# Graph layer on one Trainium2 core: SyncE fetches one gather unit in 60 instead of one in 72, node blocks travel in twos, and the store rounds of a pack become single steps

## The chip, the cores and the metric

The kernel runs on one core of one Trainium2 chip. The metric is the device time of one execution in microseconds (us); lower is better. Engine names are those of the profile: PE is TensorE (PEld its weight loads), DVE is VectorE, ACT is ScalarE, POOL is GpSimd, SP is SyncE. SP does no arithmetic here: it is a queue that issues transfers, in the order of the program.

## What is computed

One residual graph layer with a layer norm. There are 50,000 nodes of 160 numbers each (64 scalars and 32 vectors of 3) and 1,650,000 edges sorted by destination; 50,000 of them are self loops.

```python
ss, vv = (s[src], v[src])                       # the row of x at each edge's source
out0 = C0 * (ss * e0 @ W1 + dot * INV3 @ W2)    # products with the edge's 4 numbers
m = jnp.concatenate([out0, out1.reshape(-1, 3 * MUL1)], axis=1)
m_agg = jax.ops.segment_sum(m, dst, num_segments=n)
h = ...                                         # m_agg times Ws and Wv
x = _layernorm(x + relu(h))
```

## The kernel before

**Units, groups, pairs, sections.** The edges are taken in units of 128. For each unit, 128 rows of `x` must be gathered, one into each partition. Six units make a group (`G`), two groups a pair (`PG = 2`), twenty groups a section (`SG = 20`). So a pair is 12 units and a section is 10 pairs; there are 1,044 pairs and 12,522 units. The main loop (line 800) runs over pairs.

**One pair.** `gather` (line 314) has POOL fetch the rows, one indirect transfer for each unit, into a tile `xg`; the pool `rows` has four such tiles (`bufs=4`). `spread` (line 324) has VectorE make `ha`, the edge's four numbers put in the column of its destination (128 x 1536); it has three buffers, and is made for pair p+1 while pair p is in hand. `group_sums` (line 336) multiplies: twelve products (24 matmul records) of `ha` and `xg` into the PSUM tile `ps` (two buffers), and then VectorE transposes `ps` into `sums` (line 349). An `xg` tile is free again when TensorE has used it.

**Sections.** Every ten pairs `load` (line 247) has SP bring in the next section's edges, `cast` (line 265) has ScalarE make the byte offsets `ro`, and `place` (line 278) has TensorE and VectorE put them in place. The `ha` of the pairs of a section need its `place`.

**Help from SyncE.** SP fetches some units itself (`fetch`, line 665): it loads 32 offsets into registers and issues 32 transfers of one row of 640 bytes, four such batches to a unit, into a tile `xr` of the pool `far`. `HELP = {ET.SP: 72}` means one unit in 72. Lines 647 to 661 deal the four batches out over pairs (`at`) and name the pair `q` that uses the unit; here `q` is two pairs after the last batch. POOL leaves that unit out.

**Packs.** The self loops have to be taken out of the edge list. That is done in 16 packs of 128 rows of 790 edges (`pack`, line 408), one for about 60 pairs of the main loop. A pack is a list of steps: read, begin, 131 VectorE instructions (lines 438 to 528: compares, a scan, and shifts by `copy_predicated`), and 17 store rounds (`store`, line 539), each of which loads offsets into registers and issues up to 16 transfers from SP. The main loop deals a pack's steps evenly over the pairs up to its due time (lines 834 to 842); a `None` in the list is a step with nothing in it. The due pairs are 39, 99, 159, 229, 289 and so on.

**Node blocks.** 391 blocks of 128 nodes are finished along the way: `ahead` (SP loads `x` and the self-loop numbers), `own`, `nodes`, `block` (TensorE and VectorE), the norm in `norm1` to `norm3`, and `do_send` (SP writes the result). They are called a fixed number of pairs after the sums that they need (lines 794 to 798 and 843 to 850).

**Order.** Line 799 holds SP to the order of the program. The order on the other engines is made by a scheduler when the program is built, and every engine then works through its own list in order:

```python
        later_pools.enter_context(tc.manual_schedule(engines={ET.SP}))
        for p, (s, g, ng) in enumerate(pairs):
```

So an instruction of a pack may stand on VectorE's list ahead of, or behind, where its step was dealt.

Of the kernel before, what the change touches and what calls it, by code (L numbers as in the profile page):

```python
# [38 lines left out]
F32 = mybir.dt.float32  # L39
# [6 lines left out]
ET = mybir.EngineType  # L46
# [3 lines left out]
P = 128  # L50
MUL0, MUL1 = 64, 32
D = MUL0 + 3 * MUL1
NK = 4
# [13 lines left out]
PG = 2  # L67
SG = 20

HELP = {ET.SP: 72}  # L70
HEAD = 100
RP = 128
RS = 16
KM = 31
# [29 lines left out]
def tile_gnn_resnorm(ctx: ExitStack, tc: tile.TileContext, x, src, dst, attr, W1, W2, W3, W4, W5, Ws, Wv, out, n_edges):  # L104
    nc = tc.nc
    N = x.shape[0]
    NBLK, NB, GA, G, NU, NG, L, NH, NR, FAR = plan(N, n_edges)
# [83 lines left out]
    def norm2(pool, mv, n):  # L191
        rstd = pool.tile([P, 1], F32, name="rstd")
        nc.scalar.activation(rstd[:n], mv[:n, 1:2], AF.Sqrt, bias=eps_t[:n])  # L193
        return rstd

    def norm3(pool, y, mv, rstd, n):
        nc.vector.reciprocal(rstd[:n], rstd[:n])
        o = pool.tile([P, D], F32, name="o")
        nc.vector.tensor_scalar(o[:n], y[:n], mv[:n, 0:1], rstd[:n], op0=ALU.subtract, op1=ALU.mult)  # L199
        return o  # L200

# [14 lines left out]
    nblocks = math.ceil(N / P)  # L216
# [7 lines left out]

    with tc.tile_pool(name="once", bufs=1) as once, tc.tile_pool(name="raw", bufs=2) as rawp, \
            tc.tile_pool(name="idx", bufs=2) as idxp, tc.tile_pool(name="rows", bufs=4) as rowp, \
            tc.tile_pool(name="far", bufs=3) as farp, \
            tc.tile_pool(name="ops", bufs=3) as op, tc.tile_pool(name="sums", bufs=4) as sump, \
            tc.tile_pool(name="hp", bufs=alive + 4) as hpp, tc.tile_pool(name="node", bufs=3) as np_, \
            tc.tile_pool(name="ahead", bufs=7) as aheadp, \  # L230
            tc.tile_pool(name="psC", bufs=1, space=PSUM) as psC, tc.tile_pool(name="psK", bufs=2, space=PSUM) as psK, \
            tc.tile_pool(name="psP", bufs=1, space=PSUM) as psP, tc.tile_pool(name="psA", bufs=2, space=PSUM) as psA, \
            tc.tile_pool(name="psM", bufs=2, space=PSUM) as psM, ExitStack() as later_pools:
# [8 lines left out]
        dq = nc.sync  # L242
# [115 lines left out]
        def row_start(r):  # L358

            lo, hi = (math.floor(r * L * (1 - 1 / degree)) - 2 * FAR - 2, math.ceil(r * L * (1 - 1 / degree)) + 2 * FAR + 2)  # L360
            return (max(lo, 0), hi if r else 0), (max(math.floor((EH + r * L) / degree) - FAR - 2, 0),
                                                  math.ceil((EH + r * L) / degree) + FAR + 2)

        edges = dram.tile([1, (row_start(NR - 1)[0][1] + L) * C], F32, name="edges")
        selves = dram.tile([1, (row_start(NR - 1)[1][1] + W) * NK], F32, name="selves")
        edge_bytes = edges.bitcast(U8).rearrange("o f -> (o f)")
        self_bytes = selves.bitcast(U8).rearrange("o f -> (o f)")
        rows_stored = [0]
# [39 lines left out]
        def pack(c):  # L408

            r0 = c * RP  # L410
            n = min(RP, NR - r0)
            e0 = EH + r0 * L
            e = slice(e0, e0 + n * L)
            steps, T = [], {}
# [154 lines left out]


            for head, j in [(False, j) for j in range(RS)] + [(True, 0)]:
                steps += [partial(store, head, j), None, None, None]
            return steps + [stored]

        def apply_weights(at, ng):
# [8 lines left out]
        def rows_of(b):  # L584
            nb = min(P, N - b * P)
            return nb, slice(b * P, b * P + nb)

        def ahead(b):

            nb, row = rows_of(b)  # L590
            xt = aheadp.tile([P, D], F32, name="xt")
            dq.dma_start(xt[:nb], x[row, :])

            assert rows_stored[0] == NR or row_start(rows_stored[0])[1][0] >= row.stop
            sa = aheadp.tile([P, NK], F32, name="sa")
            dq.dma_start(sa[:nb], selves[0, row.start * NK:row.stop * NK].rearrange("(n k) -> n k", k=NK))
            return xt, sa

        def nodes(b):

# [47 lines left out]
        for h, (eng, period) in enumerate(HELP.items()):  # L648
            first = PG * G + h * period // 2
            nbatch = P // ROWS[eng]  # L650
            while True:
                at = [int(first + i * period / nbatch) // (PG * G) for i in range(nbatch)]
                q = at[-1] + 2
                if q >= len(pairs) or pairs[q][2] < PG:
                    break
                s, g, ng = pairs[q]
                u = (g - s * SG + ng) * G - 1 - len(helped.get(q, []))
                helped.setdefault(q, []).insert(0, (eng, h))
                for i, p in enumerate(at):
                    batches.setdefault(p, []).append((eng, h, q, s, u, i))  # L660
                first += period
# [54 lines left out]
                of_nodes[b] += (nodes(b),)  # L716

        def do_ahead(b):
            of_nodes[b] = ahead(b)

        def do_own(b):
            of_nodes[b] = own(b, *of_nodes.pop(b))
# [5 lines left out]
            rstds[b] = norm2(np_, resid[b][1], rows_of(b)[0])  # L728

        def do_store(b):  # L730
            outs[b] = norm3(np_, *resid.pop(b), rstds.pop(b), rows_of(b)[0])

        def do_send(b):
            nb, row = rows_of(b)
            dq.dma_start(out[row, :], outs.pop(b)[:nb])

        def do_cast(s):
            raws[s] = cast(raws[s])
# [179 lines left out]
    with tc.tile_pool(name="edges2", bufs=2) as ep, tc.tile_pool(name="ops2", bufs=2) as op, \  # L918
            tc.tile_pool(name="node2", bufs=1) as np_, tc.tile_pool(name="psA2", bufs=2, space=PSUM) as psA, \
            tc.tile_pool(name="psF2", bufs=1, space=PSUM) as psF:  # L920
        with tc.For_i(0, blocks, 1) as b:
            u0 = table(0, b)
            u1 = table(1, b)
            acc = np_.tile([NBLK, NK, D], F32, name="acc")
            nc.vector.memset(acc, 0.0)

            with tc.For_i(u0, u1, GA) as u:
                u = nc.s_assert_within(u, 0, NU - GA, skip_runtime_bounds_check_because="below u1")
                s_t = ep.tile([P, GA], I32, name="s_t")
                d_t = ep.tile([P, GA], I32, name="d_t")  # L930
                a_t = ep.tile([P, GA, NK], F32, name="a_t")
                e = ds(u * P, GA * P)
                nc.sync.dma_start(s_t, src1[e].rearrange("(p j) o -> p (j o)", j=GA))
                nc.sync.dma_start(d_t, dst1[e].rearrange("(p j) o -> p (j o)", j=GA))
                nc.sync.dma_start(a_t, attr[e].rearrange("(p j) k -> p j k", j=GA))
                rel = ep.tile([P, GA], F32, name="rel2")
                nc.vector.tensor_scalar(rel, d_t, base[:, ds(b, 1)], None, op0=ALU.subtract)
                xg = op.tile([P, GA, D], F32, name="xg2")
                for j in range(GA):
                    nc.gpsimd.indirect_dma_start(  # L940
                        out=xg[:, j, :], out_offset=None, in_=x,
                        in_offset=bass.IndirectOffsetOnAxis(ap=s_t[:, j:j + 1], axis=0))
                hot = op.tile([P, GA, NBLK], F32, name="hotb")
                nc.vector.tensor_tensor(hot, slots[:, :NBLK].unsqueeze(1).to_broadcast([P, GA, NBLK]),
                                        rel.unsqueeze(2).to_broadcast([P, GA, NBLK]), op=ALU.is_equal)
                xa = op.tile([P, GA, NK, D], F32, name="xa")
                nc.vector.tensor_mul(xa, xg.unsqueeze(2).to_broadcast([P, GA, NK, D]),
                                     a_t.unsqueeze(3).to_broadcast([P, GA, NK, D]))
                ps = psA.tile([NBLK, 2, 512], F32, name="ps2")
                for j in range(GA):  # L950
                    for h in range(2):
                        nc.tensor.matmul(ps[:, h, 0:2 * D], hot[:, j, :], xa[:, j, 2 * h:2 * h + 2, :],
                                         start=j == 0, stop=j == GA - 1)
                nc.vector.tensor_add(acc.rearrange("n (h k) f -> n h (k f)", h=2),
                                     acc.rearrange("n (h k) f -> n h (k f)", h=2), ps[:, :, 0:2 * D])
            parts = []
            for h in range(2):
                pt = psF.tile([D // 2, NK, P], F32, name="pt2")
                for k in range(NK):
                    nc.tensor.transpose(pt[:, k, :NBLK], acc[:, k, h * (D // 2):(h + 1) * (D // 2)], ident[:NBLK, :NBLK])  # L960
                at = np_.tile([D // 2, NK, NBLK], F32, name=f"ac{h}")
                nc.scalar.copy(at, pt[:, :, :NBLK])
                parts.append(at)
            ph = psF.tile([NBLK, D], F32, name="ph2")
            i = 0
            for h, at in enumerate(parts):
                for k in range(NK):
                    nc.tensor.matmul(ph, at[:, k, :], BWh[:, h, k, :], start=i == 0, stop=i == 2 * NK - 1)
                    i += 1
            row = ds(b * NBLK, NBLK)  # L970
            xt = np_.tile([NBLK, D], F32, name="xt2")
            nc.scalar.dma_start(xt, x[row, :])
            y, mv = norm1(np_, ph, xt, NBLK)
            o = norm3(np_, y, mv, norm2(np_, mv, NBLK), NBLK)
            nc.scalar.dma_start(out[row, :], o[:NBLK])


# [31 lines left out]
```

## Time and profile before

| | |
|---|---|
| median of 10 runs | 15,677.5 us (15,669.83 to 15,679.73) |
| the profiled execution's own time | 15,675.17 us |
| its span, first to last instruction | 15,673.4 us |
| POOL, share of the span | 75%, 12,363 instructions |
| PE | 51% |
| DVE | 40% |
| ACT | 3% |
| 16 DMA engines, mean | about 30%, 78 GB/s |

In the profile "L319" is line 319 of the kernel. A group reads: line, engine, operation, output from inputs, shape, count, then busy time and mean ns of one instruction, then the idle time of the engine just before them and what ended it. A timeline row reads: start, duration, what, and in brackets the idle time before it and its releaser. Of POOL, the time in which the gather's issue is prepared counts as idle, "issue".

### The profile page before, as it was taken

How to read it: one execution, taken by the hardware profiler on the slowest of the kernel's cores; microseconds unless marked ns; L12 is line 12 of the kernel's file. 1: busy time of each engine (PE TensorE's matmuls, PEld its weight loads, DVE VectorE, ACT ScalarE, POOL GpSimd, SP SyncE). 2: the span in 40 equal slices, each digit the busy share in tenths (PEclk: the TensorE clock that was granted, in tenths of full speed). 3: DMA queues.
4: the chain of work that ended last, by engine and by line, in shares of the span. 5: the costliest groups of instructions: out<-in, count | busy, mean ns of one | idle time of the engine just before them, and what ended most of it. 6: DMA issues, size and time to landing. Idle time of an engine off the chain costs nothing. (4 is left out here: it accounts for less than half of the span.)

```text
span 15673.4 us, 167279 instructions
## 1 busy us (share of the span) xinstructions
PE 8002.8 (51%) x38505; PEld 7272.1 (46%) x38506; DVE 6238.8 (40%) x11070; ACT 537.3 (3%) x1497; POOL 11694.9 (75%) x12363
## 2 busy tenths in 40 slices
PE   4555544554555445454554555555555455555555
PEld 3444444444444444444454444444444444444444
DVE  5342525225253442524435243352433525234322
ACT  0000000000000000000000000000000000000000
POOL 7777777777777777777777777777777777777776
PEclk7777777777777777777777777777777777777777
DMA  3323233332333323333233332323333233332322
GB/s 80 86 74 83 71 79 77 77 84 73 78 79 78 82 73 79 80 78 82 72 79 79 78 82 73 83 73 77 82 76 83 74 80 78 78 80 72 77 73 66
DMA packets 843237, 1218.89 MB, mean 78 GB/s; under 512 B 300227, under 2 KB 623912, under 8 KB 838262
## 3 DMA queue, kind: packets, MB, share of 16 engines
q0 software_dynamic: 592752, 1012.42, 26.2%
q1 hardware_dynamic: 248058, 194.45, 4.4%
q8 instruction: 323, 5.29, 0.1%
q14 instruction: 664, 5.44, 0.1%
q10 hardware_dynamic: 1440, 1.29, 0.0%
HBM read 1135.77 MB, written 71.40 MB: 77 GB/s over the span
## 5 line engine op out<-in xcount | busy, mean ns | idle before, releaser
L319 POOL DMA_INDIRECT xg<-in_x,si x12349 | 11690.7, 947 | 3933.9 <-issue 3716.4
L343 PE MATMUL ps<-xg,ha 128*128 128x160 f32 x24698 | 5310.2, 392 | 6197.7 <-DMA xg<-in_x,si 5293.9
L343 PEld LDWEIGHTS ps<-xg,ha 128*128 128x128 f32 x24698 | 5075.8, 267 | 6418.0 <-issue 5511.9
L349 DVE STREAM_TRANSPOSE sums<-ps 128x320 f32<-128x320 f32 x1044 | 535.9, 513 | 6021.2 <-PE ps L343 5939.8
L331 DVE TENSOR_TENSOR ha<-hot,pk 128x1536 f32<-128x1536 f32 x1044 | 1801.8, 1727 | 727.7 <-PE ps L343 702.3
L579 PE MATMUL phc<-BWk,sums 128*128 128x160 f32 x5220 | 923.7, 330 | 786.7 <-DVE sums L349 680.3
L579 PEld LDWEIGHTS phc<-BWk,sums 128*128 128x128 f32 x5220 | 825.8, 211 | 862.2 <-DVE sums L349 723.2
L623 PE MATMUL yx<-BWh,xT 80*128 80x320 f32 x3128 | 1003.9, 467 | 176.1 <-ACT xT L617 175.3
L627 DVE TENSOR_SCALAR t<-yx,sa 128x160 f32<-128x160 f32 x391 | 149.6, 383 | 1845.9 <-PE yx L623 1824.0
L623 PEld LDWEIGHTS yx<-BWh,xT 80*128 80x128 f32 x3128 | 598.0, 201 | 471.0 <-ACT xT L617 263.3
L639 PE MATMUL phb<-hp,hot 128*128 128x160 f32 x3474 | 605.2, 323 | 302.2 <-DVE t L629 301.4
L639 PEld LDWEIGHTS phb<-hp,hot 128*128 128x128 f32 x3474 | 536.4, 206 | 398.4 <-issue 392.4
L328 DVE TENSOR_TENSOR hot<-bank,rel 128x384 f32<-128x384 f32 x1044 | 555.1, 546 | 4.1
L629 DVE SCALAR_TENSOR_TENSOR t<-yx,sa,t 128x160 f32<-128x160 f32 x1173 | 448.2, 382 | 130.8 <-PE yx L623 105.7
L617 ACT COPY xT<-ptx 80x256 f32<-80x256 f32 x391 | 143.8, 368 | 10395.6 <-PE ptx L615 10094.5
L511 DVE COPY_PREDICATED prow<-marks,prow 128x2370 f32<-128x2370 int32 (+8 forms) x160 | 443.5, 2772 | 0.6
L511 DVE COPY_PREDICATED pra<-marks,pra 128x1580 f32<-128x1580 int32 (+8 forms) x160 | 305.0, 1907 | 0.0
L605 DVE TENSOR_TENSOR hot<-bank,rr 128x512 f32<-128x512 f32 (+2 forms) x391 | 288.3, 737 | 0.0
L640 DVE TENSOR_TENSOR phb<-phb,t 128x160 f32<-128x160 f32 x391 | 129.8, 332 | 362.4 <-PE phb L639 358.2
L581 ACT COPY hp<-phc 128x160 f32<-128x160 f32 x522 | 150.2, 288 | 2908.3 <-PE phc L579 2895.4
L193 ACT ACTIVATE rstd<-mv,eps_t 128x1 f32<-128x1 f32 x391 | 115.2, 295 | 1729.5 <-DVE mv L188 1708.2
L615 PE MATMUL ptx<-ident,xt 128*80 128x128 f32 (+1 forms) x782 | 160.0, 289 | 0.0
(148 smaller groups left out, 2858.0 us busy)
## 6 DMA issues: line engine op xcount, KB each, us to landing
xr<-in_x SPq DMA_DIRECT2D x22144, 0.6 KB
xg<-in_x,si POOLq DMA_INDIRECT x12349
edges<-prow SPq DMA_DIRECT2D x1994, 18.5 KB
r<-edges SPq DMA_DIRECT2D x99, 360.0 KB
selves<-mine SPq DMA_DIRECT2D x1992, 0.5 KB
xt<-in_x SPq DMA_DIRECT2D x390, 80.0 KB
out<-o SPq DMA_DIRECT2D x390, 80.0 KB
pra<-in_attr SPq DMA_DIRECT2D x15, 1580.0 KB
```

The source lines that it names most:

```text
L319: got.append(nc.gpsimd.indirect_dma_start(out=xg[:, j, :], out_offset=None, in_=x, in_offset=bass.IndirectOffsetOnAxis(ap=placed[0][:, u + ...
L328: nc.vector.tensor_tensor(hot[:, :n], slotsP[:, 0:W].unsqueeze(1).to_broadcast([P, n, W]), rel[:, u:u + n].unsqueeze(2).to_broadcast([P, n ...
L331: nc.vector.tensor_tensor(ha[:, :n], hot[:, :n].unsqueeze(2).to_broadcast([P, n, NK, W]), pk[:, :, u:u + n].rearrange("p k u -> p u k").un ...
L343: mm = nc.tensor.matmul(ps[:, j // G, :], ha[:, j].rearrange("p k w -> p (k w)"), xr, start=j % G == 0, stop=j % G == G - 1)
L349: nc.vector.transpose(at[:, :, i:i + ng, :].rearrange("p b g w -> p g b w"), ps[:, :ng].rearrange("p g (b f) -> p g b f", f=FB))
L511: nc.vector.copy_predicated(what[:n, a:e], mi[:, r].unsqueeze(2).to_broadcast([n, e - a, what.shape[2]]), what[:n, a + d:e + d])
L579: nc.tensor.matmul(ph[:ng * W], at[:, b, :ng].rearrange("p g w -> p (g w)"), BWk[:, b, :], start=b == 0, stop=b == ND - 1)
L605: nc.vector.tensor_tensor(hot2[:, :len(cs)], slotsP.unsqueeze(1).to_broadcast([P, len(cs), P]), rr[:, :len(cs)].unsqueeze(2).to_broadcast( ...
L615: nc.tensor.transpose(pt[:, i, :nb], xt[:nb, i * H:(i + 1) * H], ident[:nb, :nb])
L623: nc.tensor.matmul(y[:nb], xT[:, i, :nb], BWh[:, i, ks, :], start=i == 0, stop=i == 1)
L629: nc.vector.scalar_tensor_tensor(t[:nb], y[:nb, i], sa[:nb, k:k + 1], t[:nb], op0=ALU.mult, op1=ALU.add)
L639: nc.tensor.matmul(ph[:nb], hot2[:r, i, :nb], hp[:r], start=i == 0, stop=i == len(cs) - 1)
```

## The change

Six edits, in one change:

- one unit in 60 is fetched by SP (`HELP`), in the same batches of 32 rows;
- the pair that uses the unit is five pairs after the last batch (it was two); no unit is fetched for the last ten pairs; a batch is asked for no earlier than the third pair of the section before;
- the tile pool of the fetched units has four buffers (it had three);
- two node blocks share one load of `x`, one load of the self-loop numbers and one store of the result; the pool `ahead` has 5 buffers instead of 7, and the result has a pool of its own with three buffers of two blocks;
- a store round of a pack is one step; before, it was one step and three empty ones;
- `norm3` writes into a tile that it is given.

```diff
-HELP = {ET.SP: 72}
+HELP = {ET.SP: 60}
+BP = 2
...
-            tc.tile_pool(name="far", bufs=3) as farp, \
+            tc.tile_pool(name="far", bufs=4) as farp, \
...
-            tc.tile_pool(name="ahead", bufs=7) as aheadp, \
+            tc.tile_pool(name="ahead", bufs=5) as aheadp, tc.tile_pool(name="outs", bufs=3) as outp, \
...
             for head, j in [(False, j) for j in range(RS)] + [(True, 0)]:
-                steps += [partial(store, head, j), None, None, None]
+                steps.append(partial(store, head, j))
             return steps + [stored]
...
-        def ahead(b):
-
-            nb, row = rows_of(b)
-            xt = aheadp.tile([P, D], F32, name="xt")
-            dq.dma_start(xt[:nb], x[row, :])
...
+        def together(b):
+
+            bs = list(range(b // BP * BP, min(nblocks, b // BP * BP + BP)))
+            return bs if all(rows_of(i)[0] == P for i in bs) else [b]
+
+        def ahead(bs):
+
+            nb = rows_of(bs[0])[0]
+            n0, n1 = rows_of(bs[0])[1].start, rows_of(bs[-1])[1].stop
+            xt = aheadp.tile([P, BP, D], F32, name="xt")
+            dq.dma_start(xt[:nb, :len(bs)], x[n0:n1, :].rearrange("(h n) d -> n h d", h=len(bs)))
...
                 at = [int(first + i * period / nbatch) // (PG * G) for i in range(nbatch)]
-                q = at[-1] + 2
-                if q >= len(pairs) or pairs[q][2] < PG:
+                q = at[-1] + 5
+                if q >= len(pairs) - 10:
                     break
                 s, g, ng = pairs[q]
+                at = [max(a, (s - 1) * (SG // PG) + 2) for a in at]
...
         def do_store(b):
-            outs[b] = norm3(np_, *resid.pop(b), rstds.pop(b), rows_of(b)[0])
+            bs = together(b)
+            if b == bs[0]:
+                outs[b] = outp.tile([P, BP, D], F32, name="o")
+            norm3(outs[bs[0]][:, b - bs[0]], *resid.pop(b), rstds.pop(b), rows_of(b)[0])
 
         def do_send(b):
-            nb, row = rows_of(b)
-            dq.dma_start(out[row, :], outs.pop(b)[:nb])
+            bs = together(b)
+            if b == bs[-1]:
+                n0, n1 = rows_of(bs[0])[1].start, rows_of(b)[1].stop
+                dq.dma_start(out[n0:n1, :].rearrange("(h n) d -> n h d", h=len(bs)),
+                             outs.pop(bs[0])[:rows_of(b)[0], :len(bs)])
```

More of the change, by code (lines that the diff above doesn't have):

```diff
@@ L194, in norm2, with norm3 @@
         return rstd
-    def norm3(pool, y, mv, rstd, n):
+    def norm3(o, y, mv, rstd, n):
         nc.vector.reciprocal(rstd[:n], rstd[:n])
-        o = pool.tile([P, D], F32, name="o")
         nc.vector.tensor_scalar(o[:n], y[:n], mv[:n, 0:1], rstd[:n], op0=ALU.subtract, op1=ALU.mult)
@@ L586, in rows_of @@
             return nb, slice(b * P, b * P + nb)
-        def ahead(b):
-            nb, row = rows_of(b)
-            xt = aheadp.tile([P, D], F32, name="xt")
-            dq.dma_start(xt[:nb], x[row, :])
[L594 to L597, printed above, removed]
+        def together(b):
[6 more added lines that the diff above has]
+            dq.dma_start(xt[:nb, :len(bs)], x[n0:n1, :].rearrange("(h n) d -> n h d", h=len(bs)))
+            assert rows_stored[0] == NR or row_start(rows_stored[0])[1][0] >= n1
+            sa = aheadp.tile([P, BP, NK], F32, name="sa")
+            dq.dma_start(sa[:nb, :len(bs)],
+                         selves[0, n0 * NK:n1 * NK].rearrange("(h n k) -> n h k", h=len(bs), k=NK))
+            return [(xt[:, h], sa[:, h]) for h in range(len(bs))]
         def nodes(b):
@@ L718, in do_ahead @@
         def do_ahead(b):
-            of_nodes[b] = ahead(b)
+            bs = together(b)
+            if b == bs[0]:
+                of_nodes.update(zip(bs, ahead(bs)))
         def do_own(b):
@@ L730, in do_store @@
         def do_store(b):
-            outs[b] = norm3(np_, *resid.pop(b), rstds.pop(b), rows_of(b)[0])
+            bs = together(b)
+            if b == bs[0]:
+                outs[b] = outp.tile([P, BP, D], F32, name="o")
+            norm3(outs[bs[0]][:, b - bs[0]], *resid.pop(b), rstds.pop(b), rows_of(b)[0])
         def do_send(b):
-            nb, row = rows_of(b)
-            dq.dma_start(out[row, :], outs.pop(b)[:nb])
+            bs = together(b)
+            if b == bs[-1]:
+                n0, n1 = rows_of(bs[0])[1].start, rows_of(b)[1].stop
+                dq.dma_start(out[n0:n1, :].rearrange("(h n) d -> n h d", h=len(bs)),
+                             outs.pop(bs[0])[:rows_of(b)[0], :len(bs)])
         def do_cast(s):
@@ L973, in tile_gnn_resnorm @@
             y, mv = norm1(np_, ph, xt, NBLK)
-            o = norm3(np_, y, mv, norm2(np_, mv, NBLK), NBLK)
+            o = np_.tile([P, D], F32, name="o")
+            norm3(o, y, mv, norm2(np_, mv, NBLK), NBLK)
             nc.scalar.dma_start(out[row, :], o[:NBLK])
```

## The prediction

> **What bounds the kernel now.** I read the page first, then the waits of POOL, then the timelines of POOL, DVE and PE around one of its long waits, then SP's. The page's group of the gather and POOL's waits:
>
> ```profile
> L319 POOL DMA_INDIRECT xg<-in_x,si x12349 | 11690.7, 947 | 3933.9 <-issue 3716.4
> ```
>
> ```profile
> POOL xg L319 <- issue: 3716.4, 12192, 0.6
> POOL xg L319 <- PE ps L343: 164.1, 22, 23.3
> ```
>
> The reader is to see that POOL does nothing else and hardly waits: 947 ns busy and 3716.4/12192 = 305 ns of issue make a gather every 1.252 us, and 12,349 x 1.252 = 15,461 us of the 15,673. The first gather starts at 9.4, the last ends at 15,629, and 44 us of arithmetic and the last stores follow. What is left is waiting, and most of it is one entry, 164 us for PE. In POOL's timeline this falls into 15 long waits of 4 to 23 us, about 900 us apart, together 157 us beyond the normal step. One of them, in the timelines of POOL, DVE and PE:
>
> ```profile
> 1806.33 0.95 POOL L319 DMA_INDIRECT xg<-in_x,si  x1 [0.30 <-issue]
> 1827.52 0.94 POOL L319 DMA_INDIRECT xg<-in_x,si  x1 [20.25 <-PE ps L343]
> ```
>
> ```profile
> 1726.73 1.73 DVE L331 TENSOR_TENSOR ha<-hot,pk 128x1536 f32<-128x1536 f32 x1
> 1728.39 0.57 DVE L506 TENSOR_TENSOR pri<-hit,marks 128x411 int32<-128x411 int32 x1
> ...
> 1815.88 0.36 DVE L199 TENSOR_SCALAR o<-y,mv,rstd 128x160 f32<-128x160 f32 x1
> ...
> 1819.41 1.75 DVE L331 TENSOR_TENSOR ha<-hot,pk 128x1536 f32<-128x1536 f32 x1
> ```
>
> ```profile
> 1821.21 6.04 PE L343 MATMUL ps<-xg,ha 128*128 128x160 f32 x24 [3.43 <-DVE ha L331]
> ```
>
> The reader is to see a chain. VectorE ends one `ha` at 1728.5 and starts the next at 1819.4; between them stand 59 instructions of a pack. PE has gathered rows but no `ha` until 1821.2. POOL has filled all four `xg` tiles by 1807 and waits until PE frees one. So the kernel is POOL's count of gathers plus, once a pack, what a block of pack work on VectorE overruns the four tiles.
>
> **How long a block may be.** Measured gaps between those two `ha` and the excess of POOL's wait, packs 2 to 4: 79.6 gives 8.6, 90.9 gives 19.9, 85.3 gives 13.7. So about 71 us are free and each further us is a us of POOL. The free time has two parts: `ha` is finished 33 to 35 us before POOL completes its pair, and three more pairs of 15 us less the 7.5 us from `ha` to the freed tile are covered by tiles (34 + 37.5). In packs 5 to 7 VectorE came to its block later (lead 21), and 67.0, 69.5, 67.0 gave 7.3, 12.5, 7.5: the same sum.
>
> **Part one, the gathers.** The rule for `q` with 72 and 2 gives 173 units (22,144 rows / 128); with 60, 5 and the last ten pairs left out it gives 205. POOL's list in the built program has 12,317 gathers: 32 fewer, 32 x 1.252 = -40.1 us, all on the path.
>
> **Part two, where the pack's VectorE work comes to stand.** Scheduler and dealing decide this, so I take it from the order of VectorE's list in the built program, and the durations from the rows of this trace. A pack has 131 such instructions in both. Before, in the third pack, 19, 9, 3, 5, 9, 12, 6, 3, 5, 1 and 59 of them stand between one `ha` and the next; after, 12, 2, 3, 6, 5, 6, 2, 3, 2, 5 and 85. The last block grows. By the rows, all work in it takes 80.0 us before (measured gap 90.9) and 99.0 after. Over the packs the block is 99.0 us seven times, 103.9 twice, 108.6 once, 97.2 in the first pack, and 84.6 to 86.9 in five whose `ha` before has already 25 to 29 us ahead of it; before it was 77, 80, 76, then 58 to 59 with 30 to 36 ahead, 46 twice.
>
> From rows to gap: outside waits over 0.8 us, the measured gaps are about 0.97 of the row sums (rows overlap a little). The waits add 4 to 24 us before, median 11; I take 7 after, since pack instructions now stand between the steps of a node block and cover its returns from PE and ACT. So 99.0 x 0.97 + 7 = 103.
>
> Free time after: the `ha` ahead of the block now stands 7.7 us of work behind the transpose that it follows, not 2.8, so the lead falls by 5, and one of the three pairs holds a fetched unit, 1.25 less of gathering. 71 - 5 - 1 = 65. Each of the seven costs 38 us, together 266; the 103.9 and 108.6 blocks 82 and 45; the five, with leads of 19 to 23, 29 to 34 each, together 157; the first 31. Sum 581, against 157 now: +424 us.
>
> The ends: with waits of 4 in every block, 16 x 3 less, 533; with 24, 16 x 17 more, 853. Nothing in the rows lets the block cost less than its own work allows, 99.0 x 0.97 - 71 = 25 a pack or 400 in all.
>
> The Trainium skill has a rule that speaks against longer VectorE work: "SBUF — State Buffer", section "SBUF: two separate sides", says that a VectorE instruction in a two-port mode keeps GpSimd from writing the descriptors of its transfers. This trace does not show it: inside the block, 1728 to 1806, gathers follow each other every 1.250 us, and from 2800 to 2900, without pack work, every 1.251. By the page's 620 against 3100 ns, some 20 more gathers of each pack would be 2.5 us later, an estimate of 800 us over 16 packs; by the rows, 0.
>
> **Part three, SyncE.** A batch of 32 rows takes 10.4 us and 2.5 to load offsets; a store round, from the end of one batch:
>
> ```profile
> 8062.68 10.72 SPq L676 DMA_DIRECT2D xr<-in_x  x32
> 8074.79 0.29 SPq L563 DMA_DIRECT2D edges<-prow  x1
> ...
> 8080.84 0.23 SPq L563 DMA_DIRECT2D selves<-mine  x1
> ```
>
> 7.7 us, loads included. 128 more batches are 1,650 us. SP's own waits show room for them over the run, before its stores of results:
>
> ```profile
> SPq L735 <- DVE o L199: 2963.0, 145, 62.4
> ```
>
> The two-block transfers take away 3 x 195 issues of about 0.4, 234 us of SP time that nobody waits for: nothing. But the store rounds move: with 77 steps instead of 128 in a pack, the 17 rounds stand in 13.4 pairs instead of 32. There SP needs 17 x 7.7 + 10.7 x 12.9 + 5 = 274 us and has 13.4 x 14.75 = 198: it falls 76 us, 5 pairs, behind. Queued behind are the read of the next pack, the next section's edges and the fetches. The fetched unit is asked for 5 pairs ahead, and PE's list has its product behind the next pair's, so it is there in time. Edges and pack data come about 5 pairs later than now: SP stands 1.5 to 3 pairs behind POOL there today, and by the same four-tile sum I find some 27 us left. I take 0, and keep up to 15 us for each of 15 packs, 225, for the range. Below 0 it can't be, since SP comes later, never earlier.
>
> One more buffer for the units, and the earliest pair, change nothing: with 60 the users are pairs 9, 14, 19 and so on, their first batch 8 pairs before, which is inside the bound. The end after the last gather keeps its 44 us.
>
> **Sum.** Against the profiled execution, 15,675.2 (2.3 under the median): -40 + 424 = 16,059. I say 16,060.
>
> **Rivals.**
> - Faster: VectorE's blocks cost no more than now. If the scheduler's blocks found ScalarE or PE late in the old place and not in the new, or VectorE came to them earlier, POOL's waits stay at 157 and only the gathers count: 15,635; without any wait 15,478. It decides at a gap of about 75. Against it: the rows alone give 96. Chance 0.06 with all faster cases.
> - No change: the waits grow by just the 40 us saved; a gap of 78. Chance 0.03.
> - Slower by more: the store rounds are the new bound. If SP falls 7 pairs behind instead of 5, every pack gets a second wait; each pair of lag beyond that is 15 us x 15 packs = 225 us, so 16,285 for one pair and 16,510 for two. For it: the 76 us short. Against it: SP now waits before its stores, and 27 us are left. Chance 0.17.
> - My forecast, 15,880 (400 us of waits) to 16,330 (853) by its own ends: 0.74.
>
> The other cause that the change could seem to aim at, fetched units that come too late, is not in the trace: the 15 long waits all end with an `ha`.
>
> **Numbers.** The range is the forecast's own, 15,880 to 16,330; one pair of lag beyond seven, 16,285, lies inside it. Faster or slower by over 0.2%, 31 us, is about what a measurement can tell from no change: 0.06, 0.03, 0.91.
>
> **What would show it.** Right: 12,317 gathers at 1.25 us; POOL's wait for PE near 580 us in some 16 waits of 30 to 45; gaps of about 103 us between the two `ha`. Part three is wrong if a second wait follows each pack's stores, some ten pairs before the block, with SP's issue of the read seven pairs late. All is wrong if the gaps stay under 75 us.

## The result and the profile after

The kernel after takes 16,036.9 us, median of 8 runs (16,032.7 to 16,045.5), against 15,676.7 us for the kernel before (28 runs, 15,669.8 to 15,682.5). The ratio is 1.023, 95% interval 1.0221 to 1.0239. The profiled execution took 16,040.5 us, its span is 16,038.7. The forecast was 16,060.

The page's group of the gather, and the waits of POOL (total us, times, longest) in the kernel after:

```profile
L319 POOL DMA_INDIRECT xg<-in_x,si x12317 | 11657.8, 946 | 4353.6 <-issue 3704.2
```

```profile
POOL xg L319 <- issue: 3704.2, 12152, 0.3
POOL xg L319 <- PE ps L343: 435.4, 24, 47.5
POOL xg L319 <- PE ptx L622: 167.0, 14, 35.2
```

The count is the expected one and a gather still takes 946 + 305 ns. The waits for PE have grown from 164 to 435 + 167 = 602 us, the longest from 23 to 47. The second entry is no second mechanism: in five packs the profile names the transposition `ptx` as the last PE instruction ahead of the freed tile, but those waits (29 to 35 us) too end after the pack's last block. The third pack in the timelines of POOL, DVE and PE:

```profile
1875.19 0.95 POOL L319 DMA_INDIRECT xg<-in_x,si  x1 [0.30 <-issue]
1912.16 0.94 POOL L319 DMA_INDIRECT xg<-in_x,si  x1 [36.02 <-PE ps L343]
```

```profile
1801.73 1.75 DVE L331 TENSOR_TENSOR ha<-hot,pk 128x1536 f32<-128x1536 f32 x1
1803.39 0.56 DVE L506 TENSOR_TENSOR pri<-hit,marks 128x395 int32<-128x395 int32 x1
...
1837.97 5.50 DVE L528 TENSOR_REDUCE mine<-pra 128x128 f32<-128x3200 f32 x1
...
1899.98 0.36 DVE L199 TENSOR_SCALAR o<-y,mv,rstd 128x160 f32<-128x160 f32 x1
...
1904.12 1.75 DVE L331 TENSOR_TENSOR ha<-hot,pk 128x1536 f32<-128x1536 f32 x1
```

```profile
1905.92 9.36 PE L343 MATMUL ps<-xg,ha 128*128 128x160 f32 x49 [3.40 <-DVE ha L331]
```

It is the picture of before, with a longer block: `ha` ends at 1803.5, the next starts at 1904.1, 100.6 us later (before: 90.9). POOL issues its last free tile at 1875.2 and goes on 36 us later, when PE has used the new `ha`.

SP's waits of the kernel after:

```profile
SPq L679 <- ACT ro L274: 1976.9, 64, 90.1
SPq L750 <- DVE o L199: 452.8, 18, 104.4
```

In these two entries SP still waits 2.4 ms on other engines, now mostly ahead of its loads of offsets (L679) rather than ahead of its stores of results (L750). PE waited for a fetched row's tile `xr` once in the whole run, 7.2 us.

The end after the last gather changed too. The chain that ended last, first of the kernel before, then of the kernel after, from the landing of the last gathered rows:

```profile
15628.50 4.56 DMA xg<-in_x,si
15633.07 0.04 issue
15633.11 0.54 PE ps L343 x2
15633.65 0.23 PE ptx L615 x2
...
15634.38 2.42 PE yx L623 x8
```

```profile
16015.34 5.05 DMA xg<-in_x,si
16020.40 0.04 issue
16020.44 0.54 PE ps L343 x2
16020.98 1.93 PE phc L579 x10
```

Before, own products of node blocks (`ptx`, then `yx`) are still to be done when the last rows are in, and 44.0 us follow the last gather. After, PE goes straight to the last sums, and 22.4 us follow.

So the difference of the spans is accounted for: 32 gathers -40, POOL's waits beyond the normal step (those over 1.5 us from gather to gather) 606.2 - 179.6 = +426.6, the end -21.5: +365, and 16,038.7 - 15,673.4 = 365.3.

### The profile page after: what moved, and what is told of

Read it like the earlier page. It is cut to its first block, busy times and chain, and to the rows that moved or that the text cites. A ratio compares the mean times of both kernels' runs of the same rounds, so it can differ in the third digit from the quotient of the medians.

```text
span 16038.7 us, 174848 instructions
## 1 busy us (share of the span) xinstructions
PE 7969.2 (50%) x38505; PEld 7268.5 (45%) x38506; DVE 6270.1 (39%) x11070; ACT 518.0 (3%) x1497; POOL 11662.1 (73%) x12331
## 5 line engine op out<-in xcount | busy, mean ns | idle before, releaser
L630 PE MATMUL yx<-BWh,xT 80*128 80x320 f32 x3128 | 1041.3, 480 | 147.9 <-ACT xT L624 147.8
L579 PE MATMUL phc<-BWk,sums 128*128 128x160 f32 x5220 | 856.2, 314 | 207.9 <-DVE sums L349 110.4
L579 PEld LDWEIGHTS phc<-BWk,sums 128*128 128x128 f32 x5220 | 785.4, 201 | 252.8 <-issue 133.5
L285 PE MATMUL bank<-first,ones 120*128 120x20 f32 (+1 forms) x210 | 47.3, 304 | 391.4 <-DVE first L284 391.4
L285 PEld LDWEIGHTS bank<-first,ones 120*128 120x128 f32 (+1 forms) x210 | 36.5, 218 | 411.4 <-DVE first L284 411.1
```

Source lines behind the costliest of these rows:

```text
L579: nc.tensor.matmul(ph[:ng * W], at[:, b, :ng].rearrange("p g w -> p (g w)"), BWk[:, b, :], start=b == 0, stop=b == ND - 1)
L630: nc.tensor.matmul(y[:nb], xT[:, i, :nb], BWh[:, i, ks, :], start=i == 0, stop=i == 1)
```

## The experiments

**Theory**: time is the number of gathers plus what VectorE's blocks of pack work overrun the four tiles; the blocks are made where the scheduler puts instructions on VectorE's list, and any of the change's edits can shift them. **Rivals**: SP is late with what it brings; or the fetch pays as such and only the dealing harms. Each edit is shown against the kernel that its run is said to start from; `...` marks lines left out.

### Parts, on two chips where the kernel before is slower

Five runs fell on two chips on which the kernel before took 22,347 us (the first four) and 22,041 us (the fifth), so their times are not to be compared with 15,677 and only the ratios say something. What differs there is told at the end.

The fetch alone, from the kernel before:

```diff
-HELP = {ET.SP: 72}
+HELP = {ET.SP: 60}
...
-            tc.tile_pool(name="far", bufs=3) as farp, \
+            tc.tile_pool(name="far", bufs=4) as farp, \
...
-                q = at[-1] + 2
-                if q >= len(pairs) or pairs[q][2] < PG:
+                q = at[-1] + 5
+                if q >= len(pairs) - 10:
...
+                at = [max(a, (s - 1) * (SG // PG) + 2) for a in at]
```

> Only the fetch part: one unit in 60, five pairs ahead, four buffers; single node blocks and the store rounds with their empty steps as before. Theory VectorE block: the order of VectorE's list changes with it; by the rows the last pack block is 79 to 84 us in most packs (before 77 to 80 in six packs, 46 to 60 with 25 to 44 us just ahead in the others), 108 in the first. A gap of about the row sum, less 65 us free: some 18 us in each of 15 packs and 40 in the first, about 310 us of long waits against 157, less 40 us of gathers: 15,790. Theory store rounds (SyncE late is what costs): the rounds are spread as before, so the 40 us are saved and nothing comes: 15,635.

Measured: 24,435 us, ratio 1.0937 (1.0919 to 1.0956).

The dealing alone, from the kernel before:

```diff
-                steps += [partial(store, head, j), None, None, None]
+                steps.append(partial(store, head, j))
```

> Only the store rounds as single steps; one unit in 72, two pairs ahead, single blocks. Theory VectorE block: the blocks become 77 to 83 us where they were 75 to 80, and in the other packs 38 to 66 and 46 to 63 in succession where it was 24 to 44 and 46 to 60: 10 to 20 us more in each of nine packs, 3 in the others, about 290 us of long waits against 157: 15,810. Theory store rounds: SyncE falls some 50 us behind, units asked for only two pairs ahead come three pairs late, and every pack has a second long wait ahead of its block, ending with a fetched row: 15 to 30 us each, 15,900 to 16,100 and a fetched unit as releaser.

Measured: 22,477 us, ratio 1.0061 (1.0045 to 1.0078).

Only the transfers of two blocks, the pools `ahead` and `outs` with them, from the kernel before (the functions that make and send the blocks are those of the kernel after):

```diff
+BP = 2
...
-            tc.tile_pool(name="ahead", bufs=7) as aheadp, \
+            tc.tile_pool(name="ahead", bufs=5) as aheadp, tc.tile_pool(name="outs", bufs=3) as outp, \
...
```

> Only the two-block transfers with their pools. Theory VectorE block: blocks of 73 to 75 us where they were 75 to 80, nearly as before elsewhere: waits of 110 to 150 against 157, 15,630 to 15,670. Theory store rounds: 234 us less of SyncE's time on a queue that has room: 15,677, no change.

Measured: 22,248 us, ratio 0.9952 (0.9936 to 0.9969).

The change without the dealing, from the kernel after:

```diff
-                steps.append(partial(store, head, j))
+                steps += [partial(store, head, j), None, None, None]
```

> The whole change but for the store rounds, which keep their three empty steps. Theory VectorE block: the last block is 75 to 90 us by the rows (99 to 109 in the whole change): 14 to 25 us in each pack, about 300 us of long waits, 15,676 - 40 + 143 - 20 for the shorter end = 15,760. Theory store rounds: undoing the dealing takes away the whole loss: 15,635 or, with the shorter end, 15,615.

Measured: 23,989 us, ratio 1.073 (1.0712 to 1.0748).

The kernel after with VectorE, like SP, held to the order of the program:

```diff
-        later_pools.enter_context(tc.manual_schedule(engines={ET.SP}))
+        later_pools.enter_context(tc.manual_schedule(engines={ET.SP, ET.DVE}))
```

> The changed kernel, with VectorE held to the order of the program as SyncE is, so that the 131 instructions of a pack stand where they were dealt, two or three to a pair, and no block of over 20 us by the rows is left. Theory VectorE block: the 16 long waits of POOL, 580 us, go; left is the count of gathers, 12,317 x 1.252 = 15,421, 9 us before, some 20 us early waits and 20 to 45 after: 15,470 to 15,500, if VectorE in this order does not wait for TensorE elsewhere. Theory store rounds: the waits come from SyncE's 13 pairs of dense stores, which are the same: 16,000 and long waits ten pairs after each pack's stores.

Measured: 22,760 us, ratio 1.033 (1.0309 to 1.0351). PE's waits in it (total us, times, longest):

```profile
PE ps L343 <- DMA xr<-in_x: 4126.3, 127, 78.9
```

All five times were missed by thousands of microseconds, and they don't tell the theory from its rivals. There SP does not keep up: with no long block on VectorE, PE waits 4.1 ms for rows that SP fetches. The two runs with the finer fetch and the scheduler's order are 7 and 9% slower there, the run with the two-block transfers alone, fewer issues for SP, is 0.5% faster. All later runs are on chips where the kernel before takes 15,673 to 15,676 us.

### One gather tile less

```diff
-            tc.tile_pool(name="idx", bufs=2) as idxp, tc.tile_pool(name="rows", bufs=4) as rowp, \
+            tc.tile_pool(name="idx", bufs=2) as idxp, tc.tile_pool(name="rows", bufs=3) as rowp, \
```

This is the kernel after with three `xg` tiles. PE's list is the same, and VectorE's all but the same: 46 of 11,070 instructions stand elsewhere, and the sixteen last blocks hold the same rows.

> The changed kernel with three tiles of gathered rows for POOL instead of four; the order of VectorE's list and all its blocks stay the same. Theory VectorE block with four tiles to cover it: one pair less is covered, so each of the 16 long waits grows by 15 us (11 or 12 gathers of 1.25 us), from about 35 to 50: 16,037 + 240 = 16,280, and section ends with gaps over 50 us begin to wait a little, 0 to 100 more. Theory store rounds: the waits are for SyncE's rows and not for tiles: 16,037.

Measured: 16,269.2 us against 15,673.2 for the kernel before, ratio 1.038 (1.035 to 1.041). POOL's waits:

```profile
POOL xg L319 <- PE ps L343: 619.6, 28, 61.3
POOL xg L319 <- PE ptx L622: 211.5, 24, 33.9
```

A tile is worth 232 us to the kernel after, and the waits of POOL for PE grew by 229. So POOL's wait is what a pack's work overruns the tiles: a tile, 15 us of gathering, covers 229/16 = 14.3 us of a pack on average. The time came out near the 16,280 that was expected, but not in the way that was expected. The 16 long waits grew by 77 us together (555 to 632), about 5 each and not 15; the rest came ahead of them, where 17 waits of 3 to 22 us stand instead of six of 4 to 7.

### VectorE in program order

The edit is that of the fifth run above, measured again where SP issues a row in 0.32 us.

> The changed kernel with VectorE held to the order of the program, as in the run of the same edit before; there SyncE needed some 0.7 us for many of its instructions and set the pace of both kernels, so the question is still open. On a chip where SyncE issues a row in 0.32 us: theory VectorE block: no block over 20 us by the rows is left, the 16 long waits go, 15,470 to 15,500. Theory store rounds: the dense stores are the same, 16,000.

Measured: 15,450.2 us against 15,674.9, ratio 0.9856 (0.9839 to 0.9872). POOL's waits, the two largest entries:

```profile
POOL xg L319 <- issue: 3706.8, 12161, 0.3
POOL xg L319 <- DMA xg<-in_x,si: 26.6, 78, 0.9
```

Of the waits for `ps`, 0.6 us are left. The time is 20 us under the lower end of what was expected, and nothing is left in it but its parts: 7.8 to the first gather, 12,317 x 1.2504 = 15,401, 16 of waits over 1.5 us and 23 after the last gather make the span of 15,448. After the first pairs no two builds of `ha` have more than 12.3 us of rows between them (84 to 109 in the last blocks of the kernel after). This version beats both kernels.

The same on the kernel before:

> The kernel before, with its 173 fetched units and 12,349 gathers, but with VectorE's instructions kept in program order as SyncE's are. Theory (the cost of the long blocks of VectorE's list, and not the fetch, is what the time moves with): the 164 us of long POOL waits go and the end after the last gather falls by some 20 us: 12,349 gathers x 1.252 = 15,461 us plus some 30 us, about 15,490 us; the distance to the kernel after with VectorE in order (15,450 us) is then the 32 gathers alone, 40 us. Rival (the finer fetch also pays in another way, or the order helps only with transfers of two blocks and even rounds): 15,560 us or more, with PE ps waits of POOL left over 80 us.

Measured: 15,492.4 us against 15,675.8, ratio 0.9884 (0.9867 to 0.99).

```profile
POOL xg L319 <- issue: 3729.3, 12234, 1.0
POOL xg L319 <- DMA xg<-in_x,si: 22.8, 64, 1.0
```

The two runs belong together. With VectorE in order the whole change gives 15,492.4 - 15,450.2 = 42 us, and 32 gathers are 40. With the scheduler's order the same change costs 360. So the fetch does what it says, and the harm comes with the order that the scheduler makes. Its order on PE and ACT changes too when VectorE's is fixed (POOL's list does not), so these two runs alone do not name the engine; the long waits do, since they end when PE has used an `ha` that VectorE built late. An exception is the end after the last gather, which is a matter of PE's list: 44 us before, 25 here.

### Parts again

The change without the dealing (the edit of the fourth run above):

> The same edit as in the run of all but the store rounds before, where SyncE set the pace of both kernels; now for a chip where it issues a row in 0.32 us. Theory VectorE block: last block 75 to 90 us by the rows instead of 97 to 109; about 300 us of long waits in all: 15,760. Theory store rounds: the loss goes away whole, 15,635.

Measured: 15,771.3 us against 15,676.2, ratio 1.0065 (1.0042 to 1.0087).

The fetch alone (the edit of the first):

> Only the fetch part on the kernel before, again for a chip where SyncE issues a row in 0.32 us. Theory VectorE block: blocks of 79 to 89 us, 108 in the first pack; about 310 us of long waits: 15,790. Theory store rounds: they are spread as before, so the 32 gathers saved are all there is: 15,635.

Measured: 15,762.5 us, ratio 1.0057 (1.0034 to 1.0079).

```profile
POOL xg L319 <- PE ps L343: 317.0, 25, 47.2
```

The dealing alone (the edit of the second):

> The kernel before with the store rounds dealt evenly and nothing else of the change. Theory (time follows the rows that VectorE's list has between two builds of ha): in the built order seven or eight of the long blocks grow by 0 to 4 us, in the others the pack ahead holds 40 to 66 us in place of 29 to 44, 11 to 23 us more a pack; if all of that falls on POOL the sum is about +150 us, 15,830 us; if the step between the two blocks lets POOL catch up, +20 us, 15,695 us. Taken: 15,760 us. Rival (even dealing alone puts SyncE's stores late): 15,900 us or more, with POOL waits that follow SyncE's queue.

Measured: 15,773.2 us against 15,675.8, ratio 1.0062 (1.0045 to 1.0079).

```profile
POOL xg L319 <- PE ps L343: 262.2, 25, 24.1
```

The fetch alone costs 86 us, not -40: it touches no pack, yet the scheduler makes nearly all the last blocks 78 to 88 us of rows (the first 108), where they had 73 to 80 before, or 46 to 60 where they were split. POOL's waits over 1.5 us are 329 us instead of 180, the gathers -40, the end -21: +88. The dealing alone costs 97 us; its waits are 275 us, +95, and its gathers are those of before, its end nearly so (46.8 us). Its blocks are at most 83 us of rows, but in three packs one of 61 to 66 us now stands straight ahead of one of 46; these three make 53 of the 95 us. The two-block transfers on top of the fetch make 9 us, less than the intervals. Fetch and dealing alone would sum to 183 us; together with the transfers they cost 360. The blocks show it, 75 to 89 us of rows in all packs but the first without the dealing, 97 to 109 or 84 to 87 with it, and only what is over some 65 us counts. Why the scheduler makes longer blocks of the parts together was not looked into.

### A finer fetch still

The kernel after with VectorE in order and one unit in 54:

```diff
-HELP = {ET.SP: 60}
+HELP = {ET.SP: 54}
```

> The kernel after with VectorE in program order and one fetched unit in 54 in place of 60: some 23 gathers fewer, 23 x 1.252 = 29 us. Theory (SyncE has room: it issued a row in 0.32 us, a unit takes 41 us of it, and 23 more need 0.94 ms of the 2.5 ms that it waited on other engines): 15,421 us. Rival (SyncE becomes the bound: what it fetches is late where it shares a stretch with loads and stores): 15,460 us or more, with new long waits of POOL that follow PE waits on the transfer of xr.

Measured: 15,735.3 us against 15,675.8, ratio 1.0038 (1.0024 to 1.0052). The forecast of 15,421 was wrong and the rival held. PE's waits:

```profile
PE ptx L622 <- DMA xt<-in_x: 579.4, 39, 59.1
PE ps L343 <- DMA xr<-in_x: 445.3, 29, 57.2
```

With one in 60 these entries are 8.8 us and none. 23 gathers fewer are 29 us, but PE now waits up to 59 us for what SP brings, and POOL's waits over 1.5 us rise from 16 to 325. SP's total was misleading: with one in 60 it waits 2.3 ms on other engines over the run (the expectation said 2.5), but it has none to spare where it fetches, loads blocks and stores rounds in one stretch. In the 320 us from 12,800 on, in which PE waits 43 and 59 us for `xt`, SP itself waits 14 us in all. Whether rounds dealt in the old way would leave room for one in 54 was not run.

## Why the prediction was right

- **The gathers**: 12,317 at 1.251 us, -40 us. Right, and the two runs in program order show it by itself, 42 us.
- **The blocks**: predicted 581 us in 16 waits, measured 555 us in 16 waits. The gap that I took for 99 us of rows was 0.97 x 99 + 7 = 103; measured in the seven such blocks are 98 to 101. Waits of 2 to 3 us are left, not 7; that pack instructions cover more of the returns from PE and ACT is my reading of it. So the seven cost 229 us instead of 266, the two of 104 us 70 instead of 82, the one of 109 us 43 instead of 45. The free time, predicted 65, is 64 to 69. The five shorter ones were taken at 29 to 34 each, 157 in all, and measured at 33 to 34, 166. Not all of these prices follow from the rule that the prediction gives: 0.97 of the rows plus 7 less 65 makes 86 for the two of 104 us, 47 for the one of 109 and 36 for the first pack, where it says 82, 45 and 31; the sum would have been 592.
- **The first pack** was mis-sized the other way: 47 us instead of 31. Its rows were right (97.2), but its waits were 19.8 us.
- **A term that was missing**: six packs have a second, small wait of 4 to 7 us, 43 to 57 us ahead of the long one, together 36 us. PE had stood still for 38 to 42 us there, in four of the six by the profile for VectorE's transposition of `ps`, which stands in the same block, and then did the pair's products a few at a time between those of a node block. The waits outside the long ones rise from 22 us to 51, +29, and the long ones by 398 (555 - 157). So +427 stands where +424 was said because two errors of nearly 30 us cancel, -26 in the long waits and +29 outside them; that the sum comes so near is luck.
- **The end** was taken to keep its 44 us; it lost 21.5, which is nearly all of the distance from the forecast to the result. In the scheduler's order it comes with the fetch alone (22.6 us there, 46.8 with the dealing alone); with VectorE in order the kernel before has 25 us too. The row that I did not read is the chain's end of before, with the `ptx` and `yx` above: these products stood behind the last pair on PE's list.
- **SyncE**: taken as 0, with up to 225 us in the range. No second wait per pack after the stores; PE's 7.2 us for `xr` is all. The run with one in 54 shows that the rival was real and near: a tenth more fetched units, and SP sets the pace.
- **VectorE against descriptor writing** (the Trainium skill, "SBUF — State Buffer", section "SBUF: two separate sides", which would have added some 800 us by my estimate): gathers in the new, longer blocks still follow each other every 1.25 us, as the row at 1875.2 ends such a series. The trace decides for 0 again. Whether any instruction of these blocks runs in the two-port mode that the rule speaks of, no run here shows.
- **The rivals of the other side**: "blocks cost no more than now" fails at gaps of 87 to 117 us; its deciding point of 75 us fits the fetch alone, where gaps of 78 to 93 us cost 9 to 28.

## What to carry to other kernels

Where a scheduler orders an engine's list, an edit on another engine can move that list, and its price is read from the built order: sum the rows between two instructions that others wait for, and compare with the time that the buffers cover. Here that sum gave 555 of the 606 us that POOL waited; the change was worth its 40 us once VectorE was kept in program order, and that one line was worth 183 us to the kernel before. A queue's idle total does not say that it can take more; look at its busiest stretch.

## What the runs showed of the hardware

On two chips many of SyncE's instructions were slow, in the same kernel. The register move and the issue of one fetched row (min/median/max ns) in the kernel after with VectorE in order, first in its later run, then in its run on one of these chips:

```profile
L684 SPq MOVE xr<-in_x x26240: 29/29/38, 7.5 to 15114.0; - x199
L684 SPq DMA_DIRECT2D xr<-in_x x26240: 227/228/473, 7.6 to 15114.0; - x199
```

```profile
L684 SPq MOVE xr<-in_x x26240: 1/29/1412, 7.3 to 22569.7; - x199
L684 SPq DMA_DIRECT2D xr<-in_x x26240: 1/228/1454, 7.4 to 22569.7; - x199
```

The medians agree, but 7 to 8 in a hundred of the moves and issues took 699 ns or more (9 to 11 in the four runs on the other such chip). The arithmetic was not slower: `ha` took 1753 ns in both, the gather 949 against 947. In the run with only the two-block transfers VectorE's transposes waited 7.4 ms for a releaser that the profile calls "remote". The granted clock was lower in these five runs, 0.63 to 0.65 against 0.72 to 0.74 in the others; whether that is a cause or only goes with the waiting, and what makes these chips so, is not settled. It reverses the worth of a part: the finer fetch, worth 40 us elsewhere with VectorE in order, comes with 7 to 9% more time there, and the kernel after with VectorE in order, the faster of the two in-order versions elsewhere, is 3% slower than before.
